# A two-layer graph attention kernel on one core: the target's own row is added to its early sum in the projection stage, by VectorE, instead of by TensorE in the stage after it

## The chip, the cores and the metric

The kernel runs on one NeuronCore of a Trainium2 chip. The metric is the time of one execution on the device, in microseconds (us). The kernel before was timed three times: 1852.41, 1854.35 and 1872.16 us, so its median is 1854.35 us.

## The reference

Two graph-attention layers over the same 3327 x 3327 adjacency matrix, each followed by a residual and a layer norm. Only few entries of the matrix are set (about one in 200), and each node is a neighbour of itself.

```python
def gnn0(x, adj, W, a_src, a_dst):            # 8 heads of 128
    h = (x @ W).reshape(C, H, D)
    alpha_src, alpha_dst = einsum(h, a_src), einsum(h, a_dst)
    e = leaky_relu(alpha_src[:, :, None] + alpha_dst[:, None, :], 0.2)
    attn = softmax(where(adj == 0, -inf, e), axis=-1)
    return einsum('hij,hjd->hid', attn, h)    # 3327 x 1024

def gnn1(x, adj, W, a1, a2):                  # one head of 1024
    h = x @ W
    e = leaky_relu(h @ a1 + (h @ a2).T, 0.2)
    return relu(softmax(where(adj > 0, e, -9e15), axis=1) @ h)

x = layernorm(x + gnn0(x, adj, ...))
x = layernorm(x + gnn1(x, adj, ...))
```

For one target node the output is a weighted sum over its neighbours' rows, its own row among them, divided by the sum of the weights. The kernel treats the own row apart from the other neighbours (its entry is cleared from the mask), since its address needs no list.

## The kernel before

Nodes are cut into 26 tiles of 128 (`NT`); `NTH` is 13, and `EARLY` is 17. All is float32, except for masks and lists. There are three stages.

**Projection** (about 0 to 547 us of the profile). For each tile t the rows of x are turned on TensorE (L195) and multiplied with the weights (L545, 24 matmuls of 128x347 a tile). `keep` copies the result out of PSUM on ScalarE and stores rows of 1040 numbers in `h0_d`: 1024 features and 16 factors of the target-side score. Beside that, the adjacency rows are read as bytes (`load_mask`, a casting DMA from the GpSimd queue, into three buffers `masks`), counted and packed (`count`, `words`: two ScalarE passes and three VectorE operations), and turned into lists of neighbours (`listing`, seven steps a tile, most of it VectorE). From tile 13 on, a third stream, `sums_so_far`, sums the neighbours that lie in the first half of the nodes for the targets of tiles 0 to 16: blocks 0 and 1 of each target's list are gathered from `h0_d` by indirect DMAs (`fetch`), VectorE makes the weights (L677 to L681), TensorE sums 64 + 64 small matmuls into the PSUM tile `acc` (L690), and ScalarE copies it to SBUF as `z` (L738), from where it is stored in `half_d`. The sums of the weights go to `dens`.

What orders this stage is `pace()`, called 12 times for each tile (between pairs of projection matmuls; such a call is a **slot** here). In every third slot it makes one step of `counts` (clearing a mask, or counting it and loading another); it makes as many steps of `listing` as a line through given points asks for (80 of 187 steps by the slot in which tile 13 begins); and it makes one step of `sums_so_far` in each slot. Each engine works through its own instructions in that order. What is left of the streams after the last projection runs at the end of the stage.

**Layer 0** (to about 1100 us). For each of the 26 target tiles (`Layer0`): the remaining blocks are gathered (L1036: for tiles 0 to 16 blocks 2, 3 and a last one; for tiles 17 to 25 all five), five buffers of 4 x 520 KB ahead. `prepare` loads x's rows, the target's own rows of `h0_d` (`own`, L1075, 520 KB) and, for tiles 0 to 16, the early sum (`half`, L1078, 512 KB). `own` makes the own weights on VectorE (L1084 to L1090), `scale_own` scales the 8 heads of the own row on ScalarE (L1097), and `sums` adds own row and early sum to PSUM by matmuls with the identity (L1130: two of 128x512 each), between the sums of the gathered rows (L1147, L1138). `finish` divides, adds the residual, normalizes and stores y in `y_d`.

**Layer 1** (to the end). The same for 26 targets on `y_d`, with one head, and then the product with the second weights (L1290).

Between projection and layer 0 there is a branch on a flag that the lists give (the second arm, for dense graphs, isn't taken here). The buffers of the projection are given back there.

Of the kernel before, what the change touches and what calls it, by code (L numbers as in the profile page):

```python
# [9 lines left out]
F32 = mybir.dt.float32  # L10
BF16 = mybir.dt.bfloat16
U8 = mybir.dt.uint8
I32 = mybir.dt.int32
# [6 lines left out]
P = 128  # L20
# [6 lines left out]
def kernel(  # L27
# [101 lines left out]
    half_d = [scratch.tile([P, D], F32, name=f"half_d{t}") for t in range(EARLY)]  # L129
    dens = const.tile([P, EARLY, H], F32, name="dens")  # L130
    io_t = const.tile([P, P], F32, name="io_t")

    near = [const.tile([P, NG, HG], F32, name=f"near{b}") for b in range(HB)]

    class Rows:
# [376 lines left out]
    with ExitStack() as own, tc.manual_schedule():  # L512
# [14 lines left out]
        def load_mask(t):  # L527
            if t < NT:
                ads[t] = masks[t % 3]
                if t == NT - 1:  # L530
                    nc.vector.memset(ads[t].bitcast(I32), 0)
                    nc.vector.memset(ads[t][:, :1], 1.0)
                for r in pieces(t):
                    nc.gpsimd.dma_start(ads[t][r, :N], adj[at(t, r), :])
# [94 lines left out]
        def pace():  # L629

            slots[0] += 1
            n = slots[0]
            if n % 3 == 0:
                next(counts, None)
            first = 3 * total // 7
            if n <= turn_at[0]:
                aim = 4 + (first - 4) * n / turn_at[0]
            else:
                aim = first + (total - first) * (n - turn_at[0]) / (turn_at[1] - turn_at[0])
            while done[0] < aim:  # L640
                done[0] += 1
                next(steps, None)
            if soon:
                next(soon[0], None)

        def sums_so_far():
# [48 lines left out]
            def listed(s):  # L695
                re = part.sbuf("re", [P, HB * NG, H], 3)
                nc.sync.dma_start(re, re_d[s][:, : HB * NG, :])
                return re

            res = [listed(0), listed(1)]  # L700
# [11 lines left out]
            for s in range(EARLY):  # L712
                acc = part.bank("L", [P, 2, 4, DH], "part")
                made = []
                for b in range(HB):
                    n = s * HB + b
                    val = src[n % 3]
                    made.append(weights(val, b, res[0], oh))
                    yield
                    if n:  # L720
                        fetch(n + 2)
                    yield
                    sums(acc, val, b, made[b][1], range(H // 2))
                    yield
                    sums(acc, val, b, made[b][1], range(H // 2, H))
                    if b == 0:
                        yield
                        yield
# [17 lines left out]
                yield  # L746

        load_x(0)
# [18 lines left out]
        masks = [pool.tile([P, NP], U8, bufs=1, name=f"ad{n}") for n in range(3)]  # L767
        for ad in masks:
# [106 lines left out]
        for t in range(3, NT):  # L875
            load_x(t + 3)
            if 4 <= t < 4 + KT:
                nc.sync.dma_start(wt1[:, t - 4, :], w1[(t - 4) * P : (t - 3) * P, :])
            if t == 12:
                n, own_a = NT - 1, pool.tile([P, NT], I32, bufs=1, name="own")  # L880
# [8 lines left out]
            if t == 11:  # L889
                ph.iota([P, P], [[1, P]], "io_t", base=1, dst=io_t)  # L890
            if t == 16:
                nc.gpsimd.tensor_copy(loop, own_a)
# [79 lines left out]
    def sparse(own):  # L972
# [6 lines left out]
        grow = pool.tile([P, NT], F32, bufs=1, name="grow")  # L979
        grows = pool.tile([P, NT, H], F32, bufs=1, name="grows")  # L980
        nc.scalar.activation(grows, sd0[:, :, 0, :], AF.Exp, scale=1 - SLOPE)

# [76 lines left out]
        class Layer0:  # L1059
# [9 lines left out]
            def prepare(self):  # L1069
# [10 lines left out]
            def own(self):  # L1080

                t, h = self.t, self.h
                es, total = sbuf("es0", [P, 2, H], 2).rearrange("p a h -> a p h")
                nc.vector.tensor_tensor(es, grows[:, t, :], h[:, D : D + H], OP.mult)  # L1084
                nc.vector.tensor_tensor(es, es, h[:, D + H :], OP.max)
                nc.vector.tensor_scalar(es, es, loop[:, t : t + 1], None, op0=OP.mult)
                self.es = self.total = es
                if t < EARLY:
                    self.total = total
                    nc.vector.tensor_tensor(total, es, dens[:, t, :], OP.add)  # L1090

            def scale_own(self):

                h = self.h
                for n in range(H):
                    d = slice(n * DH, (n + 1) * DH)
                    nc.scalar.activation(h[:, d], h[:, d], AF.Copy, scale=self.es[:, n : n + 1])  # L1097

# [24 lines left out]
            def sums(self, b):  # L1123
# [4 lines left out]
                if j in (1, 2):  # L1128
                    for rows_ in (self.h, self.half) if self.t < EARLY else (self.h,):
                        nc.tensor.matmul(  # L1130
                            self.acc[j - 1].rearrange("p h d -> p (h d)"), ident, rows_[:, (j - 1) * HALF : j * HALF],
                            start=False, stop=False,
                        )
                elif j == 3:
# [31 lines left out]
            def finish(self):  # L1166

                ri = sbuf("ri", [P, H], 2)
                nc.vector.tensor_tensor(ri, self.den, self.total, OP.add)
                nc.vector.reciprocal(ri, ri)  # L1170
# [390 lines left out]
```

## The time and the profile before

| | |
|---|---|
| three runs | 1852.41, 1854.35, 1872.16 us |
| the profiled execution | 1778.88 us, of it 1777.1 us span |
| TensorE clock granted, mean | 0.926 |
| busy: PE, VectorE, ScalarE, GpSimd | 85%, 65%, 30%, 63% of the span |
| HBM read and written | 590.02 MB and 53.33 MB |
| DMA by queue | indirect and mask loads (q0) 458.88 MB, SyncE's (q1) 130.84 MB |

The profile is of one execution, which took 4.1% less than the median of the three timed ones (1778.88 to 1854.35). "Busy" of an engine is the time in which an instruction of it runs; the DMA share is the mean busy share of the core's 16 DMA engines. A group's row gives the line, the engine, the operation, what it writes and reads, how often, its busy time and the mean duration of one; behind the second bar stands the idle time of the engine just before such instructions, and what ended it. The shares over the whole span mix three stages with different limits, so they are read by stretch.

### The profile page before, as it was taken

To read this page: it belongs to the slowest core of one execution; us is meant where nothing else is said; L and a number is where in the kernel's file an instruction comes from. 1 tells how busy PE (TensorE), PEld (TensorE's weight loads), DVE (VectorE), ACT (ScalarE), POOL (GpSimd) and SP (SyncE) were. 2 spreads that over 40 slices of the span, in tenths; PEclk is the share of its full clock that TensorE was granted. 3 is DMA by queue.
4 is the path that set the end of the run, shared out by engine and by line. 5 is a ranking of instruction groups with operands and counts; after the bars stand their busy time and mean duration, and the time that the engine had idled before them with its cause. 6 is when DMAs were issued, how large, how long until landed. Compare 5 with 4: busy or idle time off the path is not lost.

```text
span 1777.1 us, 36731 instructions
## 1 busy us (share of the span) xinstructions
PE 1518.3 (85%) x13778; PEld 882.2 (50%) x13778; DVE 1150.6 (65%) x3125; ACT 537.5 (30%) x1602; POOL 1111.7 (63%) x1476
## 2 busy tenths in 40 slices
PE   8799999999995667666676674599999999999998
PEld 5466666666664455444554453244444444444443
DVE  6799999888873877767777775243444444444443
ACT  5678773333322233233333332011110111101110
POOL 4443358877755666656656666677676666676750
PEclk9999999999998788888788886899999999999999
DMA  7578978998888999999999999999999999999980
GB/s 195 100 138 167 163 170 302 319 314 319 296 303 331 407 411 408 394 384 406 395 397 393 385 402 365 355 395 403 396 393 386 394 390 396 401 401 395 386 345 36
DMA packets 189050, 592.41 MB, mean 333 GB/s; under 512 B 37069, under 2 KB 47079, under 8 KB 188864
## 3 DMA queue, kind: packets, MB, share of 16 engines
q0 software_dynamic: 131056, 458.88, 72.6%
q1 hardware_dynamic: 57650, 130.84, 19.8%
q8 instruction: 111, 1.82, 0.4%
q14 instruction: 75, 0.61, 0.1%
q10 hardware_dynamic: 158, 0.26, 0.0%
HBM read 590.02 MB, written 53.33 MB: 362 GB/s over the span
## 4 chain that ended last, share of the span: by engine, by line
PE 42%; DMA 18%; DVE 4%; issue 1%; ACT 1%; POOL 1%; DVEq 0%; SPq 0%; POOLq 0%; ACTq 0%
PE mm L1290 21%; PE acc L1258 13%; DMA src<-h_d,idx 7%; DMA own<-h_d 4%; PE acc L1147 3%; DMA near<-h_d,idx 3%; PE acc L1130 3%; DVE e L1115 2%; PE tr L195 1%; DMA src<-y_d,idx 1%; DMA near<-y_d,idx 1%; ACT own L1097 1%; DMA end<-h_d,idx 1%; DVE pr L1002 1%; PE acc L1138 1%
## 5 line engine op out<-in xcount | busy, mean ns | idle before, releaser
L545 PE MATMUL mm<-wt,xT 128*128 128x347 f32 (+1 forms) x1248 | 408.0, 468 | 2.1 <-DMA wt<-in_L_gnn_W_dram 1.5
L1290 PE MATMUL mm<-wt,xT 128*128 128x512 f32 x832 | 387.6, 604 | 0.0
L1036 POOL DMA_INDIRECT src<-y_d,idx x240 | 244.6, 1019 | 95.0 <-issue 32.7
L545 PEld LDWEIGHTS mm<-wt,xT 128*128 128x128 f32 x1248 | 225.7, 192 | 116.7 <-issue 18.4
L1036 POOL DMA_INDIRECT src<-h_d,idx x168 | 180.9, 1077 | 112.4 <-PE acc L1147 25.2
L1290 PEld LDWEIGHTS mm<-wt,xT 128*128 128x128 f32 x832 | 149.7, 189 | 199.1 <-issue 194.1
L1293 DVE SCALAR_TENSOR_TENSOR o<-mm,y 128x512 f32<-128x512 f32 x52 | 36.0, 692 | 317.1 <-PE mm L1290 317.1
L1036 POOL DMA_INDIRECT near<-y_d,idx x176 | 178.9, 1017 | 90.6 <-PE acc L1258 29.7
L1130 PE MATMUL acc<-own,ident 128*128 128x512 f32 x104 | 80.4, 865 | 118.8 <-ACT own L1097 115.2
L1036 POOL DMA_INDIRECT near<-h_d,idx x104 | 116.1, 1117 | 65.1 <-DMA src<-h_d,idx 13.9
L198 ACT ACTIVATE xT<-tr 128x512 f32<-128x512 f32 x104 | 63.2, 609 | 254.1 <-PE tr L195 254.0
L1272 ACT ACTIVATE z<-y,ri 128x342 f32<-128x342 f32 (+1 forms) x78 | 39.5, 569 | 300.5 <-DVE ri L1268 300.5
L660 POOL DMA_INDIRECT near<-h_d,idx x96 | 105.2, 1096 | 36.2 <-issue 24.4
L1120 ACT ACTIVATE w<-way 128x32 f32<-128x32 f32 (+1 forms) x96 | 18.5, 192 | 350.4 <-DVE e L1115 168.6
L1115 DVE TENSOR_TENSOR e<-oh,way 128x1024 f32<-128x1024 f32 x96 | 117.2, 1221 | 8.4 <-DVE way L1113 0.5
L1147 PE MATMUL acc<-src,e 128*32 128x128 f32 x2688 | 103.4, 318 | 17.6 <-DVE e L1115 17.6
L1258 PE MATMUL acc<-src,es 128*32 128x342 f32 (+1 forms) x1440 | 116.2, 454 | 0.2
L1258 PE MATMUL acc<-near,es 128*32 128x342 f32 (+1 forms) x1056 | 90.1, 476 | 28.0 <-DVE es L1249 28.0
L1147 PEld LDWEIGHTS acc<-src,e 128*32 128x32 f32 x2688 | 88.1, 129 | 47.1 <-DVE e L1115 31.9
L1147 PE MATMUL acc<-near,e 128*32 128x128 f32 x1792 | 65.8, 309 | 23.0 <-DVE e L1115 12.2
L348 ACT ACTIVATE junk<-ad 128x1664 uint8<-128x1664 uint8 x52 | 82.9, 1594 | 5.6 <-POOL ad L337 4.0
L1130 PEld LDWEIGHTS acc<-own,ident 128*128 128x128 f32 x104 | 20.4, 245 | 124.6 <-ACT own L1097 123.9
(238 smaller groups left out, 2577.8 us busy)
## 6 DMA issues: line engine op xcount, KB each, us to landing
own<-h_d SPq DMA_DIRECT2D x26, 520.0 KB
y_d<-y SPq DMA_DIRECT2D x26, 514.0 KB
y<-y_d SPq DMA_DIRECT2D x26, 514.0 KB
h_d<-ht SPq DMA_DIRECT2D x25, 520.0 KB
x<-in_x_dram SPq DMA_DIRECT2D x25, 512.0 KB
y<-in_x_dram SPq DMA_DIRECT2D x25, 512.0 KB
out_dram<-o SPq DMA_DIRECT2D x25, 512.0 KB
ad<-in_adj_dram POOLq DMA_DIRECT2D x25, 415.9 KB
```

Source lines behind the costliest of these rows:

```text
L198: nc.scalar.activation(part, tr, AF.Copy)
L348: nc.scalar.activation(junk, ad[:, n * THR : (n + 1) * THR], AF.Copy, accum_out=self.d[:, n : n + 1])
L545: nc.tensor.matmul(acc, xT[t][:, k, :], wt[:, k, CUTS0[c] : CUTS0[c + 1]], start=k == 0, stop=k == KT - 1)
L660: nc.gpsimd.indirect_dma_start(out=src[n % 3][:, g, :], out_offset=None, in_=h0_d[:THR, :], in_offset=bass.IndirectOffsetOnAxis(ap=idx[:, ...
L1036: nc.gpsimd.indirect_dma_start(out=s[:, g, :w], out_offset=None, in_=table[:n, :], in_offset=bass.IndirectOffsetOnAxis(ap=idx[:, t, b * NG ...
L1115: nc.vector.tensor_tensor(e, oh.unsqueeze(2).to_broadcast([P, ng, H, wide]), wp.unsqueeze(3).to_broadcast([P, ng, H, wide]), OP.mult,)
L1130: nc.tensor.matmul(self.acc[j - 1].rearrange("p h d -> p (h d)"), ident, rows_[:, (j - 1) * HALF : j * HALF], start=False, stop=False,)
L1147: nc.tensor.matmul(self.acc[h // 4][g * GT : (g + 1) * GT, h % 4, :], e[:, g, h, :], rowsof[:, g, h, :], start=first and h % 4 == 0, stop= ...
L1258: nc.tensor.matmul(self.acc[c][to, :m], es[:, g, :], s[:, g, CUTS[c] : CUTS[c + 1]], start=b == 0, stop=b == EB,)
L1272: nc.scalar.activation(z[:, cut], self.res[:, cut], AF.Copy, scale=ri[:, 1:2])
L1290: nc.tensor.matmul(acc, xT[:, k, :], wt1[:, k, half], start=k == 0, stop=k == KT - 1)
L1293: nc.vector.scalar_tensor_tensor(o[:, half], acc, 0.0, res[:, half], op0=OP.max, op1=OP.add)
```

## The change

For tiles 0 to 16 the own row is now handled in the projection stage. `sums_so_far` loads it from `h0_d` (`own_row`) into one of two buffers: the place of `z`, and a piece of the mask buffers. ScalarE scales its 8 heads there (`scale`), and VectorE adds the PSUM sum to it, half by half (`settle`); the result goes to `half_d`. In layer 0 these tiles load `half_d` alone, nothing is scaled, and one pair of identity matmuls is made where there were two. Tiles 17 to 25 keep load, scaling and one pair. The own weights of all tiles are made in three batches (`own_terms`), from the stored scores, in place of one tile at a time; `own_e` takes the place of `dens`, `grows` and `es0`. PSUM tile `acc` is allocated once.

Since a mask buffer is needed for the own rows, the counting step runs in two of five slots instead of one of three, a call `need(NT - 2)` stands ahead of the first early sum, the last mask lies in another buffer, and the diagonal of the adjacency matrix is read at tile 5 instead of 12. The listing is held back to 74 steps by tile 13 (2 · 187 / 5) in place of 80, and is faster after it.

```diff
-    dens = const.tile([P, EARLY, H], F32, name="dens")
+    own_e = const.tile([P, NT, H], F32, name="own_e")
...
+    def own_terms(lo, hi, mids):
+        e, score = own_e[:, lo:hi, :], sd0[:, lo:hi, 1, :]
+        for mid, scale in zip(mids, (1.0, SLOPE)):
+            nc.scalar.activation(mid, score, AF.Exp, scale=scale)
+        nc.scalar.activation(e, sd0[:, lo:hi, 0, :], AF.Exp, scale=1 - SLOPE)
+        nc.vector.tensor_tensor(e, e, mids[0], OP.mult)
+        nc.vector.tensor_tensor(e, e, mids[1], OP.max)
+        nc.vector.tensor_tensor(e, e, loop[:, lo:hi].unsqueeze(2).to_broadcast([P, hi - lo, H]), OP.mult)
...
-                ads[t] = masks[t % 3]
+                ads[t] = masks[(t + 1) % 3]
...
-            if n % 3 == 0:
+            if n * 2 % 5 < 2:
                 next(counts, None)
-            first = 3 * total // 7
+            first = 2 * total // 5
...
+            def own_row(s):
+                nc.sync.dma_start(own_rows[s % 2], h0_d[s * P : (s + 1) * P, :D])
+            def scale(s, n):
+                for h in range(4 * n, 4 * n + 4):
+                    d = slice(h * DH, (h + 1) * DH)
+                    nc.scalar.activation(
+                        own_rows[s % 2][:, d], own_rows[s % 2][:, d], AF.Copy, scale=own_e[:, s, h : h + 1]
+                    )
+            def settle(s, n):
+                half = own_rows[s % 2][:, n * HALF : (n + 1) * HALF]
+                nc.vector.tensor_tensor(half, acc[:, n].rearrange("p h d -> p (h d)"), half, OP.add)
+                if n == 1:
+                    nc.vector.tensor_tensor(own_e[:, s, :], own_e[:, s, :], den, OP.add)
+                    nc.sync.dma_start(half_d[s], own_rows[s % 2])
+            need(NT - 2)
+            own_rows = [
+                part.sbuf("z", [P, KT, P], 1, "row").rearrange("p k q -> p (k q)"),
+                ph.ads.rearrange("p a b -> p (a b)").bitcast(F32)[:, :D],
+            ]
+            acc = part.bank("L", [P, 2, 4, DH], "part")
             res = [listed(0), listed(1)]
-            for _ in range(3):
+            own_row(0)
+            for _ in range(2):
                 yield
+            own_part(0, NTH)
+            yield
...
             for s in range(EARLY):
-                acc = part.bank("L", [P, 2, 4, DH], "part")
...
+                    if b == 0 and s:
+                        settle(s - 1, 1)
                     made.append(weights(val, b, res[0], oh))
                     yield
+                    if b == 0:
+                        scale(s, 0)
...
                     sums(acc, val, b, made[b][1], range(H // 2, H))
                     if b == 0:
+                        scale(s, 1)
                         yield
+                        if s + 1 < EARLY:
+                            own_row(s + 1)
+                        if s == NTH - 3:
+                            own_part(NTH, EARLY)
                         yield
...
-                z = part.sbuf("z", [P, 2, 4, DH], 1)
-                for n in range(2):
-                    nc.scalar.activation(z[:, n], acc[:, n], AF.Copy)
-                nc.scalar.activation(dens[:, s, :], den, AF.Copy)
-                nc.sync.dma_start(half_d[s], z.rearrange("p n h d -> p (n h d)"))
+                if s == EARLY - 1:
+                    yield
+                settle(s, 0)
...
-            if t == 12:
+            if t == 5:
                 n, own_a = NT - 1, pool.tile([P, NT], I32, bufs=1, name="own")
...
-                self.h = sbuf("own", [P, HW0], 2)
-                nc.sync.dma_start(self.h, h0_d[self.t * P : (self.t + 1) * P, :HW0])
-                if self.t < EARLY:
-                    self.half = sbuf("xT", [P, KT, P], 2, "half").rearrange("p k q -> p (k q)")
-                    nc.sync.dma_start(self.half, half_d[self.t])
+                self.h = sbuf("own", [P, D], 2)
+                h0 = h0_d[self.t * P : (self.t + 1) * P, :D]
+                nc.sync.dma_start(self.h, half_d[self.t] if self.t < EARLY else h0)
             def own(self):
-                es, total = sbuf("es0", [P, 2, H], 2).rearrange("p a h -> a p h")
-                nc.vector.tensor_tensor(es, grows[:, t, :], h[:, D : D + H], OP.mult)
-                nc.vector.tensor_tensor(es, es, h[:, D + H :], OP.max)
-                nc.vector.tensor_scalar(es, es, loop[:, t : t + 1], None, op0=OP.mult)
-                if t < EARLY:
-                    nc.vector.tensor_tensor(total, es, dens[:, t, :], OP.add)
+                pass
             def scale_own(self):
-                for n in range(H):
-                    nc.scalar.activation(h[:, d], h[:, d], AF.Copy, scale=self.es[:, n : n + 1])
+                if t >= EARLY:
+                    for n in range(H):
+                        nc.scalar.activation(h[:, d], h[:, d], AF.Copy, scale=own_e[:, t, n : n + 1])
...
                 if j in (1, 2):
-                    for rows_ in (self.h, self.half) if self.t < EARLY else (self.h,):
-                        nc.tensor.matmul(...)
+                    nc.tensor.matmul(... self.h ...)
```

More of the change, by code (lines that the diff above doesn't have):

```diff
@@ L698, in listed, with own_part @@
                 return re
+            def own_part(lo, hi):
+                mid = ph.sbuf("bits", [P, 8, KMAX], 1, dt=I32).rearrange("p a b -> p (a b)").bitcast(F32)
+                m = (hi - lo) * H
+                own_terms(lo, hi, [mid[:, n * m : (n + 1) * m].rearrange("p (t h) -> p t h", h=H) for n in range(2)])
+            def own_row(s):
[18 more added lines that the diff above has]
+            acc = part.bank("L", [P, 2, 4, DH], "part")
             res = [listed(0), listed(1)]
-            for _ in range(3):
+            own_row(0)
+            for _ in range(2):
                 yield
+            own_part(0, NTH)
+            yield
             for n in range(2):
@@ L726, in sums_so_far @@
                     if b == 0:
+                        scale(s, 1)
                         yield
+                        if s + 1 < EARLY:
+                            own_row(s + 1)
+                        if s == NTH - 3:
+                            assert scored.issuperset(range(EARLY))
+                            own_part(NTH, EARLY)
                         yield
@@ L746, in sums_so_far @@
                 yield
+            settle(EARLY - 1, 1)
         load_x(0)
@@ L766 @@
             nc.tensor.matmul(avs[:, n, :], one, arow[n // 2][:, half], start=True, stop=True)
-        masks = [pool.tile([P, NP], U8, bufs=1, name=f"ad{n}") for n in range(3)]
+        ph.ads = pool.tile([P, 3, NP], U8, bufs=1, name="ad")
+        masks = [ph.ads[:, n, :] for n in range(3)]
         for ad in masks:
@@ L890 @@
                 ph.iota([P, P], [[1, P]], "io_t", base=1, dst=io_t)
-            if t == 16:
+            if t == 11:
                 nc.gpsimd.tensor_copy(loop, own_a)
@@ L979, in sparse @@
         grow = pool.tile([P, NT], F32, bufs=1, name="grow")
-        grows = pool.tile([P, NT, H], F32, bufs=1, name="grows")
-        nc.scalar.activation(grows, sd0[:, :, 0, :], AF.Exp, scale=1 - SLOPE)
+        own_terms(EARLY, NT, [pool.tile([P, NT - EARLY, H], F32, bufs=1, name=f"mid{n}") for n in range(2)])
         ys = [pool.tile([P, HW], F32, bufs=1, name=f"y{n}") for n in range(3)]
@@ L1073, in prepare, with scale_own @@
                 load_rows(self.y[:, :D], x, self.t)
-                self.h = sbuf("own", [P, HW0], 2)
-                nc.sync.dma_start(self.h, h0_d[self.t * P : (self.t + 1) * P, :HW0])
-                if self.t < EARLY:
-                    self.half = sbuf("xT", [P, KT, P], 2, "half").rearrange("p k q -> p (k q)")
-                    nc.sync.dma_start(self.half, half_d[self.t])
+                self.h = sbuf("own", [P, D], 2)
+                h0 = h0_d[self.t * P : (self.t + 1) * P, :D]
+                nc.sync.dma_start(self.h, half_d[self.t] if self.t < EARLY else h0)
             def own(self):
+                pass
+            def scale_own(self):
                 t, h = self.t, self.h
-                es, total = sbuf("es0", [P, 2, H], 2).rearrange("p a h -> a p h")
-                nc.vector.tensor_tensor(es, grows[:, t, :], h[:, D : D + H], OP.mult)
-                nc.vector.tensor_tensor(es, es, h[:, D + H :], OP.max)
-                nc.vector.tensor_scalar(es, es, loop[:, t : t + 1], None, op0=OP.mult)
-                self.es = self.total = es
-                if t < EARLY:
-                    self.total = total
-                    nc.vector.tensor_tensor(total, es, dens[:, t, :], OP.add)
-            def scale_own(self):
-                h = self.h
-                for n in range(H):
-                    d = slice(n * DH, (n + 1) * DH)
-                    nc.scalar.activation(h[:, d], h[:, d], AF.Copy, scale=self.es[:, n : n + 1])
+                if t >= EARLY:
+                    for n in range(H):
+                        d = slice(n * DH, (n + 1) * DH)
+                        nc.scalar.activation(h[:, d], h[:, d], AF.Copy, scale=own_e[:, t, n : n + 1])
             def begin(self):
@@ L1128, in sums @@
                 if j in (1, 2):
-                    for rows_ in (self.h, self.half) if self.t < EARLY else (self.h,):
[L1130 to L1133, printed above, removed]
+                    nc.tensor.matmul(
+                        self.acc[j - 1].rearrange("p h d -> p (h d)"), ident, self.h[:, (j - 1) * HALF : j * HALF],
+                        start=False, stop=False,
+                    )
                 elif j == 3:
@@ L1168, in finish @@
                 ri = sbuf("ri", [P, H], 2)
-                nc.vector.tensor_tensor(ri, self.den, self.total, OP.add)
+                nc.vector.tensor_tensor(ri, self.den, own_e[:, self.t, :], OP.add)
                 nc.vector.reciprocal(ri, ri)
```

## The prediction

> **What bounds the kernel now.** First the 40 slices of the span (44.4 us each), since shares of the whole span mix stages:
>
> ```profile
> PE   8799999999995667666676674599999999999998
> DVE  6799999888873877767777775243444444444443
> DMA  7578978998888999999999999999999999999980
> GB/s 195 100 138 167 163 170 302 319 314 319 296 303 331 407 411 408 394 384 406 395 397 393 385 402 365 355 395 403 396 393 386 394 390 396 401 401 395 386 345 36
> ```
>
> Three regimes are to be seen: TensorE at nine tenths for twelve slices, then DMA at nine or more with TensorE at six, then both. The second view is busy time by stretch: tiles 13 to 25 of the projection (the first list of an early sum is loaded at 250.0 us, the last projection matmul ends at about 547), layer 0, layer 1. Columns are start:end, length, busy time of PE, PEld, DVE, ACT and POOL with counts, clock, DMA share, GB/s.
>
> ```profile
> 250.00:547.00 297.00, 277.30 (x3143) 187.02 (x3142) 247.10 (x665) 106.14 (x401) 219.70 (x377) 0.99 0.87 304
> 570.00:1100.00 530.00, 355.53 (x5730) 259.07 (x5730) 394.62 (x988) 165.59 (x484) 338.52 (x313) 0.80 1.01 393
> 1100.00:1777.00 677.00, 644.24 (x3693) 276.88 (x3693) 291.39 (x867) 79.41 (x164) 435.56 (x429) 0.98 0.94 366
> ```
>
> Layer 0 is held by the DMA engines: share 1.01, no other engine above 75% (DVE 394.62 of 530). The projection's second part is held by TensorE (93%), with VectorE at 83% and DMA at 0.87 not far behind. The third view is who waits in layer 0 (600 to 1090 us), the fourth its groups, the fifth its transfers:
>
> ```profile
> PE acc L1130 <- ACT own L1097: 110.5, 23, 13.9
> DVE es L1084 <- DMA own<-h_d: 41.6, 16, 13.2
> ...
> L1097 ACT ACTIVATE own<-own,es 128x128 f32<-128x128 f32 x200 | 60.8, 389 | 0.0
> L1130 PE MATMUL acc<-half,ident 128*128 128x512 f32 x68 | 47.6, 792 | 0.0
> ...
> q0 software_dynamic: 41738, 145.19, 75.5%
> q1 hardware_dynamic: 15972, 47.43, 25.1%
> own<-h_d SPq DMA_DIRECT2D x23, 520.0 KB
> half<-half_d SPq DMA_DIRECT2D x15, 512.0 KB
> ```
>
> TensorE waits 110.5 us for scaled own rows, yet the DMA engines don't pause meanwhile, so that wait is mostly a consequence: own rows arrive late because transfers queue. Bytes set this stage.
>
> **What the Trainium skill says.** "DMA: Bandwidth & Descriptors", section "Issuing engines are not separate DMA queues": transfers started by SyncE and by GpSimd run on the same 16 engines and interleave. The trace agrees: the two queues' shares in layer 0 add up to 75.5 + 25.1%. "Perfetto Trace Analysis", section "Optimization Strategy" (under Identifying Performance Opportunities): where the contended engine changes over time, interleaving the regimes may help. That is what the change amounts to; the trace shows the regimes, not yet the help. "VectorE: DVE Perf Modes", section "The TRN2 errata": a float32 tensor_tensor takes (N + 151) / 0.96 ns, 691 ns for 512 columns; the trace has 692 ns for 128x512 with a PSUM operand (L1293) and 681 ns without (L1052).
>
> **The change, part by part.** Times are against the profiled execution (1778.88 us: span 1777.1 and 1.8 around it).
>
> 1. *Layer 0 loses transfers.* 17 loads of `own` of 128 x 1040 x 4 = 532,480 bytes go, and the 9 left shrink by 8 KB: 9.13 MB. At the stage's 393 GB/s that is **23.2 us**; at the best slice's 411 GB/s it is 22.2. By the queue's own time (25.1% of 490 us for 47.43 MB, 386 GB/s) it is 23.7. All on the path, as the stage is DMA-bound. Also gone: 34 identity matmuls (27 us of PE at 792 ns), 136 scalings (17 x 2.44 us, the measured length of a set of eight), and VectorE's own-weight operations: 26 x (167 + 170 + 238 ns) and 17 x 167 ns, 17.8 us. These lie beside DMA, so I cost them at nothing; the cover is the share of 1.01. `own` is no longer waited for by VectorE and ScalarE, only by TensorE; next late are the gathers, as now. Taken: -23; bounds -30 (a third of the gap between 393 and 411 GB/s, 23 us over the stage, also comes back through earlier freed buffers) and -15 (a third of the bytes turns into idle DMA time).
>
> 2. *The projection's second part gains the same transfers.* 17 x 524,288 = 8.91 MB. SyncE's transfers from 400 to 540 us took 17.8% of 140 us for 9.36 MB, 376 GB/s; so 23.7 us of all engines. Share: (0.87 x 297 + 23.7) / 297 = 0.95.
>
> 3. *VectorE there.* 34 `settle` additions at 692 ns: 23.5 us. 17 additions of 8 columns at about 0.2: 3.4. Two batches of own terms, six small operations: 1.5. Listing: six steps come over from ahead of tile 13. The listing's groups there sum to some 187 us for 14.5 tiles of seven steps, 1.84 us a step, so 11. Sum 39.4; busy 247.1 + 39.4 = 286.5 of 297, **96%**. Of the 50 us that VectorE idles there now, 16.6 are waits for lists from TensorE (kq, L495) and 14.1 for gathers (L677). The first go when VectorE is later; the second stay and grow with the DMA share: I add 5. So 286.5 + 14 + 5 = 306: **+9 us**. If all fits into idle time: 0. Upper bound: 22, if the 16.6 us of list waits stay too in good part.
>
> 4. *ScalarE there.* 34 evictions (L738, 600 ns, in pairs of 1.08 us: 18.4) and 17 copies go; 17 x 2.44 = 41.5 us come. 106 + 22 = 128 of 297: hidden by ScalarE's own idle time.
>
> 5. *New waits.* `settle` waits for the own row's load, the scaling and the sums; behind it in VectorE's queue stand the next marks, weights and listing steps, and TensorE waits for the weights. On SyncE's queue `own_row(s + 1)` waits until `half_d` of s - 1 is stored, with x loads, `h0_d` stores and list stores behind it. A target takes 9 slots of 297 / 152 = 1.95 us, 17.6 us. `settle(s - 1, 1)` and its store come in slot 0, `own_row(s + 1)` in slot 4, its scaling in slots 10 and 12. With 10 us for a row's transfer in the congested stage (chain pieces of 8.5 to 10.3 us), it is issued at 10 us and there at 20, against slot 10 at 19.5: just in time. In the less congested projection I take 6 us (the one drained `half_d` store at its end is waited for 4.9), so nothing is added. x loads have more than a tile of lead. Cost 0; bounds 0 and 17 x 2 = 34.
>
> 6. *First part.* Masks come every 5 slots instead of 6. Two loads now take 16.44 us (a tile), the software queue 57.1% of it, so its share becomes 69%, DMA there about 0.98 from 0.87. ScalarE, with 3.56 us a mask and 81% busy from 120 to 180 us, goes to about 90%. TensorE holds that part at 99%; less listing helps VectorE (92%) by 11 us. By tile 13 about 53 counting steps have been made and 44 are needed, so `need` adds no stall. +1; bounds -2 and +6. The diagonal's tiny transfers only move.
>
> 7. *Seams.* 165 in place of 164 steps for 152 slots: the 23 us between last projection and layer 0 keep their form. VectorE's two additions replace ScalarE's copies; three batched operations more at the start of layer 0: +1; bounds 0 and +4.
>
> Sum: -23 + 9 + 0 + 1 + 1 = **-12 us** of 1778.88, or 0.7%. Scaled to the median by 1854.35 / 1778.88 it is -12.5: **1842 us**.
>
> **The rivals.** *A, all hidden:* the projection keeps its length and layer 0 takes the whole -30: 1854 - 31 = 1823. For it: 50 us of idle VectorE and 13% of idle DMA cover both; and in slower executions TensorE may be what is slow, with more cover. Against it: both end near 95%, with in-order queues. *B, slower:* `settle` ties VectorE to TensorE, ScalarE and the row load; a wait of w per target costs 17 w, since VectorE has 4% left to catch up. It decides from w = 0.7 us (12 / 17); with w = 2 us it is 34 - 12 = +22, 1877. For it: the row is just in time by step 5, and gathers are waited for already. Against it: rows are double-buffered, halves are settled one slot after their sums. *C, no relief:* layer 0 is held by the loop of gather buffers (free, gather, sum), not by bytes, and the engines count as busy while transfers merely wait; then it gains 5, the rest costs 11: +6, 1860. For it: GpSimd waits for TensorE's sums before gathers (25.2 us). Against it: 393 GB/s of a best 411.
>
> **The numbers.** Main case 0.47 (own range 1830 to 1853), A 0.23, B 0.20, C 0.10. About 1%, 18.5 us, is what a measurement of this kernel can tell from no change. Faster by more: A, and 30% of the main case, 0.37. Slower: B, 0.20. Within: 0.43. The range takes in A and most of B, and the scatter of the runs (to 1872): 1820 to 1876.
>
> **What would show it.** Layer 0 at about 507 us where it took 530, still at DMA share 1.0; VectorE at 95% and DMA at 0.95 between tile 13 and the last projection, which is some 10 us longer; waits of L677 for gathers above 14 us. Step 5 is wrong if `settle` shows waits of more than a microsecond a target; step 1 if the DMA share of layer 0 falls below 0.97; step 6 if the first part is longer. If a clock below 0.99 is granted in the projection, it is another case.

## The result, and the profile after

The kernel after took 1879.33 us (median of 12 runs, 1873.01 to 1885.86), the kernel before beside it 1855.11 us (12 runs, 1851.7 to 1872.16): a ratio of **1.0118**, 95% interval 1.0099 to 1.0138, so 1.2% slower. Forecast were 1842 us in a range of 1820 to 1876.

The profiled execution of the kernel after took 1883.85 us, in line with its timed runs. That of the kernel before had taken 1778.88, 4% below its own. The two profiles are therefore not of one condition, and may not be subtracted. First the slices of the kernel after, 47 us each:

```profile
PE   8799998888897577787787777599999999999998
DVE  6689897778875576766666786334443444444443
DMA  7589967778887999999989999799999999999990
GB/s 184 96 133 168 196 219 262 265 263 291 294 299 257 346 371 352 400 332 362 399 320 368 404 378 381 286 376 384 382 382 374 383 380 378 395 389 381 368 355 34
```

TensorE is at seven and eight tenths in layer 0 now, and the DMA rate there is mostly 320 to 400 GB/s. Then busy time by stretch: first list of an early sum to last projection matmul, layer 0 (from its first loads to the last store of y), layer 1 (columns as in the prediction):

```profile
252.00:610.00 358.00, 306.01 (x3173) 201.66 (x3172) 277.20 (x746) 128.58 (x506) 220.47 (x394) 0.94 0.81 278
637.00:1192.00 555.00, 419.00 (x5662) 277.55 (x5662) 380.56 (x895) 129.48 (x352) 338.62 (x318) 0.85 0.97 369
1192.00:1882.00 690.00, 665.20 (x3693) 286.39 (x3693) 286.34 (x856) 77.64 (x161) 422.20 (x422) 0.98 0.92 350
```

The projection's second part is 61 us longer than in the profile that the prediction read, and layer 0 is 22 us longer though it has fewer transfers and fewer matmuls. What holds TensorE in layer 0 is seen in its timeline (start, length, operation, count, in brackets the idle time before it and what ended it):

```profile
704.56 1.72 PE L1185 MATMUL acc<-src,e 128*32 128x128 f32 x46
706.54 0.46 PE L1185 MATMUL acc<-src,e 128*32 128x128 f32 x4 [0.27 <-issue]
707.29 0.45 PE L1185 MATMUL acc<-src,e 128*32 128x128 f32 x4 [0.29 <-issue]
708.00 0.46 PE L1185 MATMUL acc<-src,e 128*32 128x128 f32 x4 [0.26 <-issue]
```

The 64 small matmuls of a block start as a run of 46, and then come in fours, each 0.7 us after the one before, with nothing in the profile that they wait for ("issue"). I call these **gaps**. In the waits of layer 0 (total, times, longest, us) they are TensorE's largest entry by far, and the wait for scaled own rows is down to 2.1 us:

```profile
PE acc L1185 <- issue: 100.9, 270, 1.1
...
PE acc L1168 <- ACT own L1136: 2.1, 1, 2.1
```

The prediction's profile of the kernel before has 1.3 us of such waits ahead of matmuls in layer 0. So two questions: did the change bring the gaps, and what of the 1.2% is the change?

### The profile page after: what moved, and what is told of

It is laid out like the page before. It is cut to its first block, busy times and chain, and to the rows that moved or that the text cites. A ratio compares the mean times of both kernels' runs of the same rounds, so it can differ in the third digit from the quotient of the medians.

```text
span 1882.1 us, 36498 instructions
## 1 busy us (share of the span) xinstructions
PE 1630.6 (87%) x13710; PEld 924.0 (49%) x13710; DVE 1155.2 (61%) x3090; ACT 521.8 (28%) x1559; POOL 1094.9 (58%) x1476
## 4 chain that ended last, share of the span: by engine, by line
PE 53%; issue 7%; DVE 3%; DMA 2%; another core or an unknown queue 1%; POOL 0%; ACT 0%; DVEq 0%; SPq 0%; POOLq 0%; ACTq 0%
PE mm L1328 19%; PE acc L1296 13%; PE acc L1185 12%; PE acc L1176 4%; PE acc L1168 3%; PE tr L205 1%; DVE pr L1051 1%; DMA near<-y_d,idx 1%; PE den L1196 1%; DMA own<-h_d 1%; DMA end<-y_d,idx 0%; DMA av<-in_L_gnn_a_dram 0%; DVE e L1154 0%; DVE y L1213 0%
## 5 line engine op out<-in xcount | busy, mean ns | idle before, releaser
L555 PE MATMUL mm<-wt,xT 128*128 128x347 f32 (+1 forms) x1248 | 416.0, 476 | 4.4 <-DMA wt<-in_L_gnn_W_dram 3.3
L1085 POOL DMA_INDIRECT src<-y_d,idx x240 | 240.5, 1002 | 118.3 <-PE acc L1296 51.8
L555 PEld LDWEIGHTS mm<-wt,xT 128*128 128x128 f32 x1248 | 230.2, 195 | 122.3 <-issue 26.3
L1328 PEld LDWEIGHTS mm<-wt,xT 128*128 128x128 f32 x832 | 149.5, 189 | 199.4 <-issue 194.6
L1085 POOL DMA_INDIRECT src<-h_d,idx x168 | 176.9, 1053 | 98.5 <-issue 34.8
L1185 PE MATMUL acc<-src,e 128*32 128x128 f32 x2688 | 152.1, 291 | 65.9 <-issue 62.2
L1185 PE MATMUL acc<-near,e 128*32 128x128 f32 x1792 | 109.4, 303 | 51.2 <-issue 38.6
L1296 PE MATMUL acc<-src,es 128*32 128x342 f32 (+1 forms) x1440 | 128.1, 455 | 3.5 <-issue 1.2
L1296 PE MATMUL acc<-near,es 128*32 128x342 f32 (+1 forms) x1056 | 98.2, 475 | 21.9 <-issue 11.4
L1185 PEld LDWEIGHTS acc<-near,e 128*32 128x32 f32 x1792 | 65.4, 120 | 99.7 <-issue 91.4
L700 PE MATMUL part<-near,e 128*32 128x128 f32 x1408 | 62.1, 308 | 34.7 <-DVE e L691 26.2
```

The lines of the kernel that those rows point to most:

```text
L555: nc.tensor.matmul(acc, xT[t][:, k, :], wt[:, k, CUTS0[c] : CUTS0[c + 1]], start=k == 0, stop=k == KT - 1)
L700: nc.tensor.matmul(acc[g * GT : (g + 1) * GT, h // 4, h % 4, :], e[:, g, h, :], vals[:, g, h, :], start=b == 0 and h % 4 == 0, stop=b == H ...
L1085: nc.gpsimd.indirect_dma_start(out=s[:, g, :w], out_offset=None, in_=table[:n, :], in_offset=bass.IndirectOffsetOnAxis(ap=idx[:, t, b * NG ...
L1185: nc.tensor.matmul(self.acc[h // 4][g * GT : (g + 1) * GT, h % 4, :], e[:, g, h, :], rowsof[:, g, h, :], start=first and h % 4 == 0, stop= ...
L1296: nc.tensor.matmul(self.acc[c][to, :m], es[:, g, :], s[:, g, CUTS[c] : CUTS[c + 1]], start=b == 0, stop=b == EB,)
L1328: nc.tensor.matmul(acc, xT[:, k, :], wt1[:, k, half], start=k == 0, stop=k == KT - 1)
```

## The experiments

The runs were made in five groups, with the kernel before timed in each: e1 to e4 (chip 5 by the record's number) and e5 to e8 (chip 8), where it took 1891 us; e9 to e12 (chip 14), e13 to e16 (chip 8 again) and e17 and e18 (chip 14), where it took 1780 to 1782 us. The profiles of the first two groups have gaps, those of the last three have none. Number 8 stands in both kinds, so the chip's number doesn't decide whether there are gaps. Ratios are to the kernel before of the same group, with 95% intervals. Some variants compute less, as said at each. Lengths of stages are read as above, from one profile of each run. With gaps, single profiles of the same code differ by up to 13 us in the projection and by 9 us in layer 0; without gaps by 4 us in the projection.

### Did the change bring the gaps?

**e1**, the kernel before, unchanged:

> The kernel before, unchanged, for a second profile. Its first profiled execution took 1779 us where twelve timed ones took 1852 to 1872, so it may not be typical. Theory P (the profile was untypical: TensorE issued its small matmuls without gaps there): the new profile is near 1855 us, with gaps of 0.2 to 0.5 us between groups of 3 to 5 matmuls of the gathered rows in layer 0, and a DMA share below 1 there; then the 12 us of slowing are to be sought by stage against this profile. Theory C (the change itself brought the gaps): the new profile shows none, and layer 0 is again 530 us long at a DMA share of 1.0.

1882.53 us. Its stretches are again the projection's second part and layer 0:

```profile
253.40:585.20 331.80, 300.30 (x3143) 196.55 (x3142) 247.23 (x666) 107.21 (x401) 214.26 (x377) 0.95 0.80 272
610.80:1179.80 569.00, 434.96 (x5730) 282.77 (x5730) 398.38 (x989) 167.45 (x489) 334.89 (x319) 0.85 0.98 376
```

Of TensorE's waits between 640 and 1170 us the first two are

```profile
PE acc L1147 <- issue: 86.2, 207, 1.2
PE acc L1130 <- ACT own L1097: 13.3, 11, 2.3
```

Theory P holds (the time is in line with the 1891 us of this group, not with the 1855 that it named). The same program that took 297 and 533 us there takes 332 and 569 us here. The gaps come without the change, and TensorE waits only 13.3 us for scaled own rows, where the first profile had 110.5. The first profile was true, but of another condition than the timed runs.

### Schedule or eviction?

**e2**, the kernel before with the schedule of the kernel after (three of its edits; the place of the last mask and the reading of the diagonal are changed with them):

```diff
-            if n % 3 == 0:
+            if n * 2 % 5 < 2:
-            first = 3 * total // 7
+            first = 2 * total // 5
+            need(NT - 2)
```

> The kernel before with the schedule of the kernel after alone: counting in two of five slots, listing to 74 steps by tile 13, masks ended before the first early sum, diagonal at tile 5. Theory S (schedule costs: more list work on VectorE beside the early sums): 8 to 15 us slower than before. Theory V (VectorE's additions and their waits cost): within 4 us of before.

**e3**, the kernel after with the first two of these lines turned back:

> The kernel after with the schedule of the kernel before (counting in one of three slots, listing to 80 steps by tile 13). Theory S: it is 8 to 15 us faster than the kernel after, so about 10 us slower than before. Theory V: within 4 us of the kernel after, 20 to 28 us slower than before.

**e4**, the kernel before, evicting on VectorE:

```diff
-                    nc.scalar.activation(z[:, n], acc[:, n], AF.Copy)
-                nc.scalar.activation(dens[:, s, :], den, AF.Copy)
+                    nc.vector.tensor_copy(z[:, n], acc[:, n])
+                nc.vector.tensor_copy(dens[:, s, :], den)
```

> The kernel before, with the eviction of the early sums (two halves and the sums of weights) copied by VectorE in place of ScalarE, and nothing else. Theory V in its form 'an eviction on VectorE ties its queue to TensorE': 10 to 20 us slower than before. Theory R (the cost lies in the own rows' load and scaling, not in the engine that evicts): at most 5 us slower, the price of 34 copies in idle time.

| | ratio | interval | last projection matmul | layer 0 |
|---|---|---|---|---|
| e2 schedule alone | 1.0013 | 0.9979 to 1.0046 | 597.9 us | 563 us |
| e3 after, old schedule | 1.0068 | 1.0046 to 1.0091 | 614.0 us | 562 us |
| e4 VectorE evicts | 1.0101 | 1.0053 to 1.0148 | 611.3 us | 560 us |

The schedule costs nothing that can be told. Moving 34 copies from ScalarE to VectorE, with no own row loaded, scaled or added, costs 1.0%, 19 us of 1891. VectorE's waits at the copy of the sums come to 46.5 us in six entries of the projection's second part, 18.6 of them for TensorE's last sums of weights; its waits for lists fell meanwhile, from 57.5 us (e1) to 23.8. What lengthens the stage is seen at TensorE, whose longest wait ahead of the early sums in e4 is this (weights on VectorE, then the matmuls that use them):

```profile
447.95 1.22 DVE L681 TENSOR_TENSOR e<-oh,w 128x1024 f32<-128x1024 f32 x1
449.28 1.08 PE L690 MATMUL part<-near,e 128*32 128x128 f32 x16 [4.94 <-issue]
```

The profile calls it issue, but it ends 0.1 us after the weights do, and so do all waits there of over 1.3 us in e4. TensorE's waits of over 0.5 us that end so, whatever their name, come to 28.5 us in e4 and to 4.9 in e1: 24 us more, for a last projection matmul that is 26 us later. e3 is 13 us slower than before, between the two theories' figures; against e5, in the next group, it is 4 us ahead of the kernel after, with intervals that overlap.

### What sets layer 0 where there are gaps?

**e5**, the kernel after where there are gaps:

> The kernel after, unchanged, on the same chip as the next three. Theory L (lock-step: VectorE waits in settle for TensorE's sums, and TensorE then waits for the weights that stand behind settle in VectorE's queue): 1.0 to 1.4% slower than before, with some 40 us of VectorE waits at the settle line and 25 us or more of TensorE waits for the early weights, in a projection that is some 25 us longer; layer 0 gives back less than 15 us.

1.0092 (1.0066 to 1.0119). Last projection matmul at 612.7 us, layer 0 562.2 us.

**e7**, no load, weighing and scaling of own rows in layer 0 for tiles 0 to 16, matmuls kept; **e8**, loads kept, matmuls left out (the own rows' part is missing from both results):

```diff
-                    for rows_ in (self.h, self.half) if self.t < EARLY else (self.h,):
+                    for rows_ in (self.half, self.half) if self.t < EARLY else (self.h,):   # e7, and no load
+                    for rows_ in (self.half,) if self.t < EARLY else (self.h,):             # e8
```

> The kernel before, in which layer 0 doesn't load, weigh and scale the own rows of tiles 0 to 16 (their own terms are left out of sum and divisor); the matmuls with the identity stay, with the early sum added twice. Theory D (layer 0 is set by bytes, as the prediction took it): 20 to 25 us faster than before. Theory T (in a typical execution it is set by TensorE, which issues its small matmuls with gaps): at most 8 us faster.

> The kernel before, in which the own rows of tiles 0 to 16 are loaded, weighed and scaled in layer 0, but not added (the 34 identity matmuls of 128x512 are left out, and with them the own rows' part in the sum). Theory D: within 5 us of before. Theory T: 34 x 0.6 to 0.8 us, 15 to 27 us, faster than before.

e7 gave 0.9992 (0.9957 to 1.0027): 9 MB fewer bring nothing. e8 gave 0.9936 (0.9905 to 0.9968), 12 us by the ratio; less than the 15 to 27 expected, so the price of a matmul that is left out was put too high, but clear of zero. Where TensorE has gaps, layer 0 is set by its stream and not by bytes: in e7 TensorE's busy time and its issue waits at the gathered rows, 436.4 and 103.0 us, fill 539 of 560.5 us (624.5 to 1185). One thing doesn't fit. The kernel after leaves out these loads and as many matmuls, and yet its layer 0 took 555 to 562 us (result, e3, e5) where the unchanged one took 560 to 569 (e1, e2, e4), a difference no larger than the scatter. In e5 the issue waits at the gathered rows are 107.2 us, in e1 they are 88.5; why they grow isn't shown.

### Can settle be put better?

**e6**, both halves behind the next target's first weights, one slot later:

```diff
-                    if b == 0 and s:
-                        settle(s - 1, 1)
                     made.append(weights(val, b, res[0], oh))
                     yield
                     if b == 0:
+                        if s:
+                            settle(s - 1, 0)
+                            settle(s - 1, 1)
                         scale(s, 0)
...
-                if s == EARLY - 1:
-                    yield
-                settle(s, 0)
```

> The kernel after, with both halves of settle put behind the next target's first weights, one slot later (the slot left free ahead of the last target's settle goes as well). The same work on every engine, only later in VectorE's queue. Theory L: the waits of VectorE at settle fall below 15 us and those of TensorE for early weights below 12 us, and the kernel is 12 to 30 us faster than the kernel after. Theory W (VectorE's added work and the own rows' transfers and scaling as such cost): within 5 us of the kernel after.

1.0068 (1.0036 to 1.0100), by the medians 4.7 us faster than e5, which is theory W's figure; the last projection matmul is at 612.8 us, as late as in e5. The waits, though, fell as theory L said. Of TensorE's waits between the first list and that matmul, in e5 the largest was

```profile
PE part L700 <- DVE e L691: 37.5, 15, 7.1
```

and in e6 it has shrunk to the last of these lines, while the eviction itself came in its place:

```profile
PE part L700 <- issue: 16.7, 32, 2.9
PE dd L783 <- issue: 6.2, 15, 0.5
PE part L700 <- DVE ad L727: 6.1, 3, 2.7
PE part L700 <- DVE row L727: 4.8, 3, 3.2
PE part L700 <- DVE e L691: 4.4, 2, 3.4
```

So theory L's microseconds didn't come back: 33 us of one wait went, 11 us of another came, and issue waits ahead of L700 and of the sums of weights rose by 14 (22.9 in e6, 8.5 in e5). That leaves some 8 us less waiting, and TensorE's busy time rose by 13.

**e9**, first half ahead of those weights and second half behind them, both in that slot:

```diff
                     if b == 0 and s:
-                        settle(s - 1, 1)
+                        settle(s - 1, 0)
                     made.append(weights(val, b, res[0], oh))
+                    if b == 0 and s:
+                        settle(s - 1, 1)
```

> The kernel after, with the first half of settle right ahead of the next target's first weights and the second half right behind them, both in that slot (between the kernel after and the late settle). Theory E (one PSUM tile: VectorE, busy and in order, either waits for TensorE's sums when its eviction stands early, or makes TensorE wait for the bank when it stands late): within 6 us of the kernel after and of the late settle, the last projection matmul at 605 us or later. Theory L (only the place in the queue is wrong): 12 us or more faster than the kernel after, the last projection matmul before 600 us.

In this group there were no gaps, so its times in us can't be held against the expectation's. 0.9971 (0.9959 to 0.9983): 0.3% faster than before.

**e10**, ScalarE evicting and GpSimd adding (load and scaling of the own row stand later, too):

```diff
-                nc.vector.tensor_tensor(half, acc[:, n].rearrange("p h d -> p (h d)"), half, OP.add)
+                    nc.scalar.activation(zc[:, n * HALF : (n + 1) * HALF], acc[:, n].rearrange(...), AF.Copy)
+                nc.gpsimd.tensor_tensor(own_rows[s % 2], own_rows[s % 2], zc, OP.add)
```

> The kernel after, with ScalarE evicting the early sums to a buffer of their own, as before, and GpSimd adding the scaled own rows to them (17 additions of 128x1024 at 2.4 us, behind the gathers of a slot); the last mask is counted ahead of the first early sum too, since its buffer is taken. VectorE is out of it. Theory E: the projection is as long as before (last projection matmul at 585 to 600 us), and the kernel is 14 to 26 us faster than the kernel after, so 0 to 9 us faster than before. Theory W (own rows' loads and scalings cost, whoever evicts): within 6 us of the kernel after.

1.0106 (1.0087 to 1.0126): a miss. The last projection matmul ends at 587.4 us, 37 us later than the 550 of the kernel before without gaps, while layer 0 is 509 us. The projection was the longest of all runs without gaps, so "any engine but VectorE" is no cure. And VectorE wasn't out of it:

```profile
585.02 2.36 POOL L733 TENSOR_TENSOR row<-row,ad 128x1024 f32<-128x1024 f32 x1
585.38 2.06 DVE L687 TENSOR_TENSOR w<-near,re 128x32 f32<-128x32 f32 x1 [2.71 <-DMA near<-h_d,idx]
```

The operation at L687 takes 0.18 us in the median; here it begins during an addition on GpSimd (POOL) and ends with it. Of VectorE's operations that overlap one of the 17 additions, 11 are longer than their median by more than 0.2 us, and all together by 23.7 us. TensorE, moreover, waited 19.8 us for GpSimd's small results (dd, from more_b), against 2.9 in the first profile. So e10 doesn't test theory E; how the 37 us divide between these two and the later scaling isn't separated.

**e11** and **e12** try the gain without the projection: the kernel before, with early sum and scaled own row added in SBUF in layer 0, and one pair of identity matmuls.

```diff
                     nc.scalar.activation(h[:, d], h[:, d], AF.Copy, scale=self.es[:, n : n + 1])
+                if self.t < EARLY:
+                    nc.gpsimd.tensor_tensor(h[:, :D], h[:, :D], self.half, OP.add)   # e12: nc.vector
```

> The kernel before, with the early sum added to the scaled own row by GpSimd in layer 0 (17 additions of 128x1024 at 2.4 us), and one pair of identity matmuls in place of two for tiles 0 to 16. Theory T (layer 0 is set by TensorE's stream): 6 to 12 us faster than before, as where those matmuls were left out. Against it: GpSimd's additions wait for the scaling ahead of gathers in its queue; then 0 to 10 us slower.

> The same with VectorE adding (17 additions at 1.2 us). Theory T: 4 to 10 us faster than before. If VectorE's wait for loads and scaling holds the next weights up, as settle does in the projection: 3 to 15 us slower.

1.0011 (1.0002 to 1.0020) and 1.0011 (1.0003 to 1.0020), layer 0 at 535 us in both: as long as before. Without gaps one pair of matmuls in place of two brings nothing here. It isn't e8 under the other condition, though: the additions stand in the matmuls' place, and TensorE waited for them, 145.1 us in e11 and 96.9 in e12.

### What is it worth without gaps?

**e13**, the kernel after, **e14**, the kernel of e9, **e15**, the kernel of e7, and **e16**, the kernel of e4, all in one group, where before took 1782 us:

> The kernel after, unchanged. Theory G (the sign depends on gaps in TensorE's issue): on a chip where the kernel before takes about 1780 us, without gaps, 0.2% slower to 0.8% faster than before, layer 0 some 24 us shorter and the projection 15 to 22 us longer; on a chip where it takes 1850 us or more, with gaps, 0.9 to 1.2% slower, layer 0 at most 10 us shorter. Theory N (it is slower everywhere): 0.9% slower or more on either.

> The kernel after with the halves of settle around the next target's first weights. Theory G: on a chip without gaps 0.3% faster than before, as in its first run; on a chip with gaps 0.4 to 0.9% slower than before. Theory N, with the place of settle as the cause: 0.3% faster on either.

> The kernel before without load, weighing and scaling of the own rows of tiles 0 to 16 in layer 0, the identity matmuls kept, with the early sum added twice (their own terms are left out of sum and divisor). Theory G: 20 to 25 us faster than before on a chip without gaps, within 5 us of before on a chip with gaps.

> The kernel before with VectorE copying the early sums out of PSUM in place of ScalarE. Theory G: 14 to 22 us slower than before on a chip with gaps; 5 to 15 us slower on a chip without gaps, where TensorE's list results come earlier and VectorE has less idle time to lose and to give. Theory N: the same 19 us on either.

| | no gaps: ratio | interval | with gaps: ratio |
|---|---|---|---|
| kernel after | 1.0005 (e13) | 0.9991 to 1.0019 | 1.0092 (e5), 1.0118 (result) |
| VectorE evicts alone | 1.0041 (e16) | 1.0021 to 1.0060 | 1.0101 (e4) |
| own rows not loaded in layer 0 | 0.9872 (e15) | 0.9849 to 0.9895 | 0.9992 (e7) |
| settle around the weights | 0.9962 (e14) | 0.9948 to 0.9977 | not run |

Theory G's figures without gaps hold in every row (those with gaps are the runs it was made from). The sign doesn't turn for the kernel after: it is slower or level. For the eviction alone the two intervals still touch. The same missing loads are worth 1.3%, 23 us, or nothing. Layer 0 of the kernel before (first profile), of the kernel after and of the kernel of e15, without gaps:

```profile
572.60:1105.40 532.80, 355.53 (x5730) 259.07 (x5730) 398.35 (x989) 166.98 (x488) 341.01 (x315) 0.80 1.01 395
```
```profile
597.40:1105.80 508.40, 320.30 (x5662) 251.41 (x5662) 382.06 (x896) 128.14 (x353) 338.01 (x314) 0.82 1.02 395
```
```profile
577.40:1089.10 511.70, 345.67 (x5730) 258.44 (x5730) 386.19 (x921) 128.04 (x353) 336.48 (x316) 0.82 1.01 394
```

The DMA engines stay full in all three, at 394 to 395 GB/s, and the time follows the bytes. The same kernel with gaps, in the same stage (e7):

```profile
624.40:1194.50 570.10, 436.50 (x5730) 281.86 (x5730) 385.74 (x921) 129.00 (x353) 337.36 (x319) 0.85 0.96 359
```

Fewer bytes, and the rate falls in their place, to 359 GB/s at 0.96. What the kernel after pays for its 24 us is in the projection's second part:

```profile
252.40:572.50 320.10, 283.41 (x3173) 190.98 (x3172) 277.54 (x746) 128.97 (x507) 227.62 (x394) 0.98 0.89 312
```

The last matmul ends at 572.5 us, where the projection of the kernel before has 546.9 to 551.3 in four profiles without gaps (before, e11, e12, e15). VectorE's idle time ahead of settle, by what ended it (total and times, e13):

```profile
  PE dd L782: 10.1, 6
  ACT re L495: 7.6, 3
  PE part L700: 3.0, 1
```

and TensorE's waits for the early weights, in the first profile, in e13, and in e14, whose last matmul is at 563.8 us:

```profile
PE part L690 <- DVE e L681: 9.7, 7, 2.3
```
```profile
PE part L700 <- DVE e L691: 35.3, 20, 2.6
```
```profile
PE part L700 <- DVE e L691: 14.5, 8, 2.4
PE part L700 <- DVE row L727: 6.8, 5, 1.9
PE part L700 <- DVE ad L727: 4.8, 5, 1.9
```

Here the place of settle does count: 9 us of waiting less, and the projection 9 us shorter. Counted as in e4, by when a wait ends, the waits for early weights are 9.7 to 11.9 us in those four profiles, 20.1 in e16 (last matmul at 560.5 us, 10 us later) and 34.9 in e13 (22 us later).

**e17** and **e18**, the kernel of e9 once more, and with the old schedule (the two lines of e2 turned back):

> The kernel after with the halves of settle around the next target's first weights, once more. On a chip without gaps (before about 1780 us): 0.3 to 0.4% faster than before. On a chip with gaps (before 1850 us or more): theory G, 0.4 to 0.9% slower.

> The same with the schedule of the kernel before (counting in one of three slots, listing to 80 steps by tile 13). Theory S (the schedule is part of the loss: fewer list steps are left beside the early sums): 4 to 10 us faster than the run beside it. Theory V (only the eviction on VectorE counts): within 3 us of it.

Again without gaps: 0.9969 (0.9959 to 0.9979) and 0.9953 (0.9935 to 0.9970); medians 1774.84 and 1772.31 us against 1779.75. The schedule is worth 2.5 us by the medians, with intervals that overlap, as theory V said. Both are faster than the kernel before, by 0.3 and 0.5%; against the kernel after the comparison within one group is e14 with e13, 7.7 us faster by the medians. Neither was run where there are gaps, so whether they beat the kernel before there stays open.

## Why the prediction was wrong

Wrong was first its ground: **the first profile's 1778.88 us stood 4% below the timed runs, and the prediction scaled this by a factor** as if every stage were longer alike. With gaps the bound of layer 0 is another one. (No profile of the kernel before was taken at 1855 us; that it had gaps there follows from e1 and from the profile after.) Two steps failed: step 1, whose 23 us didn't come where TensorE has gaps, and step 5, which put the new waits at nothing. By its steps:

**Step 1.** *Layer 0, -23 us, "bytes set this stage".* Right where the premise holds: 532.8 to 508.4 us, -24.4 (e13), and e15 has it alone. In the condition of the timed runs the step failed: with gaps layer 0 took 569.0, 562.9 and 559.8 us unchanged (e1, e2, e4) and 555.0, 562.0 and 562.2 with the change (result, e3, e5), -4 by the means and within the scatter. The DMA share, 0.98 in e1 for 1.01 in the first profile, hardly tells the two conditions apart. There "gone beside DMA, cost nothing" is turned round: loads cost nothing (e7), matmuls cost (e8). Rival C had the outcome (layer 0 doesn't follow its bytes) and named the loop of gather buffers. e7 and e8 point to TensorE's stream; its sums are a part of that loop, and no run separates the two.

**Step 2.** *DMA share in the projection, 0.95.* 0.89 without gaps, 0.81 with; TensorE's waits there weren't for transfers.

**Step 3.** *VectorE's added work, +9 us.* The work was put too high (and the 16.6 us of list waits that the step puts down to TensorE end, in the trace, with ScalarE's copies of the lists): VectorE's busy time rose by 30 us (247.1 to 277.5), not 39, and with the step's 14 and 5 us of waits that makes 296.5, no more than the 297 us of before. Yet the projection became 22 us longer without gaps (550.0, the mean of four, to 572.5) and about 20 with (592.5, the mean of e1, e7 and e8, to 612.7 in e5). It wasn't work that cost. Nor was it the granted clock, 0.95 in e1 and in e5 alike, and 0.98 in e13 and in e15.

**Step 5.** *New waits, cost 0, bounds 0 and 34.* This step failed, and rival B was right: without gaps VectorE idles 20.7 us ahead of settle and TensorE waits 35.3 us for weights, 25.6 more than the 9.7 of the first profile. 22 us over 17 targets is 1.3 us each; B decides from 0.7. Of what B ties VectorE to, TensorE's sums ended most of the idle time (13.1 us); 7.6 ended with a step of the listing on ScalarE (`re`), and the row that is "just in time", B's main reason, doesn't show. e16 has half of it (10 us) without any own row, e14 gets 9 us back by the place in the queue alone.

**Steps 4, 6 and 7.** *ScalarE hidden, first part +1, seams +1.* Right as far as can be told: ScalarE was busy for 129.0 us in e13, 128 were forecast; the first list is loaded at 252.4 us in e13 and at 250.0 to 255.4 before, the seam is 24.9 us for 25.7, and e2 has the schedule at 1.0013.

Sum without gaps: -24 + 22, and 1.0005 was measured. Sum with gaps: -4 + 20, which is 0.8% of 1891 where 0.9% was measured (e5); each term is known no better than the scatter of single profiles, so that this agreement is in part luck. Rival A's argument that slower executions give TensorE's cover to both was the wrong way about: they took the gain away.

The price of 691 ns that the prediction took from the Trainium skill, "VectorE: DVE Perf Modes", section "The TRN2 errata", stood: settle's additions took 672 to 692 ns. The interleaving of regimes, from "Perfetto Trace Analysis", section "Optimization Strategy", gave its 24 us only where the regime was the one in the profile.

Left open: what makes the gaps, and why they come at some times and not at others. The profile calls them issue and names no releaser. As far as the record goes, three things are no answer. A lower granted clock isn't it: in layer 0 it was 0.80 in the first profile and 0.85 in e1. The loading of instructions looks alike: 1.82 MB on their queue (q8), 0.4% of the DMA engines' time, in both. And the chip alone isn't it, if number 8 was the same chip both times, which isn't on record. Why late settle (e6) gained nothing in the projection with gaps isn't settled either.

## What to carry to other kernels

When the profiled execution doesn't take the time of the timed runs, take another profile before believing its bound: the same load was worth 1.3% in one condition and nothing in the other. An eviction is better put on an engine that idles when it falls due, as ScalarE did here (30% busy). On VectorE (65%), which works through its instructions in order, 23 us of copies cost 7 to 19 us, as it waited for TensorE's sums and then TensorE for its weights. Where the eviction must be there, try the first half ahead of and the second half behind the work that the producer waits for next: here, without gaps, 0.9962 for 1.0005.

## What the runs showed that I had not expected

TensorE can issue small matmuls in bursts of three to five with 0.2 to 0.5 us between them, after a run of some 40, with nothing to wait for in the profile: about 90 us of waits ahead of matmuls in layer 0 at one time, 1 us at another, with one program. The kernel before then takes 1891 or 1780 us. And an addition on GpSimd can hold VectorE: with 17 of them, 40 us in all, in VectorE's place, operations of VectorE that overlapped them lasted 23.7 us longer, and the projection grew by 37 us (e10), more than by any eviction on VectorE. Beside the additions of e11, in layer 0, they lasted 34.5 us longer.
